# Seven quarter-block products in place of four block products, for two units of a feed-forward layer at a time

## The chip, the cores and the metric

The kernel runs on one core of a Trainium2 chip. The metric is the device time of one execution in microseconds (us), lower is better. The engines are TensorE (PE; its weight loads are shown apart as PEld), VectorE (DVE), ScalarE (ACT), GpSimd (POOL) and SyncE (SP, which here only issues DMAs). Each engine runs its own instructions in order, and waits on semaphores for the others. Matmul results lie in PSUM, in eight banks of 128 partitions x 512 f32; everything else lies in SBUF.

## The reference

`x` is 1,024 tokens of 512 channels. Two layers are added to it, each a conditioner with low-rank adapters followed by a gated feed-forward network:

```
c = down(silu(gate(x)) * up(x))        # conditioner 0: width 1,376, each of its 3 weights plus an adapter per batch
x = x + down(silu(gate(c)) * up(c))    # ffn 0: width 1,792, each weight w * (su @ sv), su and sv of rank 4
l = x @ W.T + b + adapter(x)           # conditioner 1: 512 to 512
x = x + down(silu(gate(l)) * up(l))    # ffn 1: width 1,792, int4 weights with a scale per 128 inputs
```

## The kernel before, in words

Tokens lie on the free axis, in two halves of `TB` = 512; channels lie on the partitions, in four chunks of 128 (`KC`). The hidden width of a layer is cut into *units* of 128: 11 for conditioner 0 (`c`), 14 for ffn 0 (`f`), 14 for ffn 1 (`q`). The program runs through these stages, one after the other: units of `c` (`gate_up` with adapters), `down` of `c` to `h`, units of `f` (`gate_up`), `down` of `f` onto `x`, conditioner 1 (`l_main`, `l_finish`), units of `q`.

**Seven products.** In `c` and `f`, a unit's gate rows and up rows against the two halves of the tokens, and two halves of the input channels, form a 2 x 2 block product, which is done in seven block products in place of eight (in Winograd's arrangement). Product i multiplies a form of the weights, a[i] (128 rows, 256 channels), with a form of the tokens, b[...] (256 channels, 512 tokens). So it is two matmul calls of 128 x 128 weights and 512 columns in f32, and each call leaves two records in the profile. `weight_forms` (L278 to L285) makes s1 = a21 + a22, s2 = s1 - a11, s4 = a12 - s2 and, in the place of a21, s3 = a11 - a21; for `c` from unit 3 on and for `f` it runs on GpSimd (`gate_up_forms`). `token_forms` (L287 to L309) makes T3, T1, T2, T4 on VectorE, once for a layer. `gate_up` (L434 on) does products 1, 6, 7, 5, 3, 2, 4 on TensorE, each into a PSUM bank of its own; ACT copies product 1 (L462), VectorE adds the sums together (L471 to L498), ACT does the SiLU (L495, L499), and GpSimd multiplies gate and up (L497, L502). `down` (L508 on) does the same with pairs of units: its weight forms (`ds`) and token forms (`dt`, L532) are made by VectorE, in the order 1, 2, 3, 7, 5, 6, 4.

**Preparing a unit.** `prepare` loads a unit three ahead (SP's queue) and finishes a unit two ahead. In `f`, `finish_f` (L402 to L420) first makes the scales su @ sv: 12 matmuls (`pw`, 16 rows, 128 columns, f32r, from `scale_parts`, in three banks), which VectorE multiplies into the gate and up weights (L415, twice) and the down weights (L419); then GpSimd makes the forms.

**Conditioner 1** (L852 to L896) is a plain product: four output chunks by two token halves by four input chunks, 32 f32 calls, in PSUM tiles of two banks, plus the low-rank adapter (`low_rank`, `expand`). `l_finish` splits the result into two f32r parts, hi by ACT (L880) and lo by VectorE (L881), which the units of `q` read (L904).

**Order.** A tile is a slot of a pool; a tag with one buffer (`bufs` = 1) is reused only when all readers of its last tile are done. `in_order` pins an instruction behind the one traced before it on its engine; without it the scheduler of the compiler may move an instruction ahead where its operands come early.

Of the kernel before, what the change touches and what calls it, by code (L numbers as in the profile page):

```python
# [7 lines left out]
F32 = mybir.dt.float32  # L8
# [5 lines left out]
P = 128  # L14
# [26 lines left out]
def kernel(  # L41
# [40 lines left out]
    wgu_pool = pool(left0, "wgu", "left", AHEAD + 2)  # L82
# [172 lines left out]
    def expand(banks, b, columns, ts, fresh=(), more=()):  # L255

        for turn in range(len(banks)):
            for tb in range(NTB):  # L260
                i = (turn + tb) % len(banks)
                if banks[i][tb] is None:
                    continue
                rows = bass.ts(tb, P // NTB)
                mm(
                    banks[i][tb], b[rows, columns[i] : columns[i] + P], ts[i][rows, :],
                    start=(i, tb) in fresh, stop=(i, tb) not in more,
                )
# [10 lines left out]
    def weight_forms(engine, a11, a12, a21, a22, s1, s2, s4, pinned=False):  # L279

        in_order(engine.tensor_tensor(s1, a21, a22, ALU.add))
        for to, x1, x2 in ((s2, s1, a11), (s4, a12, s2), (a21, a11, a21)):
            made = engine.tensor_tensor(to, x1, x2, ALU.subtract)
            if pinned:
                in_order(made)  # L285

    def token_forms(pool, name: str, src, pinned: bool, then=None):  # L287
# [9 lines left out]
        for t, x1, x2 in (  # L297
            ("T3", "22", "12"), ("T1", "12", "11"), ("T2", "22", "T1"), ("T4", "21", "T2")
        ):
            b[t] = []  # L300
            for k in range(K2):
                to = pool.tile([P, TB], F32, tag=f"{t}{k}", name=f"{t}_{name}{k}")
# [8 lines left out]
    def product(ps, a, b, start: bool, stop: bool):  # L311
        for n, (w, src) in enumerate(zip(a, b)):
            mm(ps, w, src, start=start and n == 0, stop=stop and n == len(b) - 1)
# [3 lines left out]

    def load_c(f: int, after=None):
        wgu = wgu_pool.tile([P, 2, KC, P], F32, tag="wgu", name=f"wgu_c{f}")
        if after is not None:  # L320
            in_order(nc.vector.tensor_copy(wgu[:, 0, 0, 0:1], after[:, 0:1]))
        if f:
            in_order(nc.sync.dma_start(out=wgu, in_=c_gu[f]))
        wd = wd_pool.tile([P, H], F32, tag="wd", name=f"wd_c{f}")
        ready["c", f] = wgu, wd

    def load_c_down(f: int):
        in_order(nc.sync.dma_start(out=ready["c", f][1], in_=c_down[f]))

    def gate_up_forms(layer: str, f: int, engine):  # L330
        wgu, wd = ready[layer, f][:2]
        s = wgu_pool.tile([P, 3, KC // 2, P], F32, tag="s", name=f"s_{layer}{f}")
        k1, k2 = slice(0, KC // 2), slice(KC // 2, KC)
        g, u = wgu[:, 0], wgu[:, 1]
        weight_forms(engine, g[:, k1], g[:, k2], u[:, k1], u[:, k2], *(s[:, i] for i in range(3)))
        a = {
            1: g[:, k1], 2: g[:, k2], 7: u[:, k1], 4: u[:, k2],
            5: s[:, 0], 6: s[:, 1], 3: s[:, 2],
        }
        ready[layer, f] = {i: [w[:, k] for k in range(KC // 2)] for i, w in a.items()}, wd  # L340

    def finish_c(f: int):
        gate_up_forms("c", f, nc.vector if f < 3 else nc.gpsimd)

# [53 lines left out]
    def load_f(f: int):  # L398
        wgu = wgu_pool.tile([P, 2, KC, P], F32, tag="wgu", name=f"wgu_f{f}")
        in_order(nc.sync.dma_start(out=wgu, in_=f_gu[f]))  # L400
        wd = wd_pool.tile([P, H], F32, tag="wd", name=f"wd_f{f}")
        in_order(nc.sync.dma_start(out=wd, in_=f_down[f]))  # L402
        ready["f", f] = wgu, wd

    def finish_f(f: int):
        wgu, wd = ready["f", f]

        pw = [bank(f"pw_{f}_{s}") for s in range(3)]
        for k in range(KC):
            for s in range(3):  # L410
                rows, ks = slice(s * G, s * G + 4 * RS), bass.ts(k, P)
                sv, su = scale_parts[rows, ks], scale_parts[rows, H + f * P : H + (f + 1) * P]
                mm(pw[s][:, ks], *((su, sv) if s == 2 else (sv, su)), start=True, stop=True)
        for s in range(2):
            nc.vector.tensor_tensor(  # L415
                wgu[:, s].rearrange("p k f -> p (k f)"),
                wgu[:, s].rearrange("p k f -> p (k f)"), pw[s], ALU.mult,
            )
        nc.vector.tensor_tensor(wd, wd, pw[2], ALU.mult)  # L419
        gate_up_forms("f", f, nc.gpsimd)  # L420

    units = [("c", f) for f in range(NF0)] + [("f", f) for f in range(NF)]
    load = {"c": load_c, "f": load_f}
    finish = {"c": finish_c, "f": finish_f}

    def prepare(layer: str, f: int):

        n = units.index((layer, f))
        for ahead, do in ((AHEAD, load), (AHEAD - 1, finish)):
            if n + ahead < len(units):  # L430
                which, at = units[n + ahead]
                do[which](at)
# [4 lines left out]
    def gate_up(  # L437
        act_pool, temps, layer: str, f: int, b, adapters=None, first=False, last=False, between=()
# [3 lines left out]
        a = ready[layer, f][0]  # L442
        mul = (nc.vector if last else nc.gpsimd).tensor_tensor

        def temp(what: str):
            return temps.tile([P, TB], F32, tag=what, name=f"{what}_{layer}{f}", bufs=2)
# [10 lines left out]
        def of(i: int, src: str, stop: bool = True):  # L457
            ps[i] = new(i)
            product(ps[i], a[i], b[src], True, stop)
            return ps[i]  # L460

# [16 lines left out]
        add(u, ps[5], u, ALU.add)  # L478
        for do in between[:1]:
            do()  # L480
        if not first:
            of(3, "22", done)
        for do in between[1:]:
            do()
        if not first:
            of(2, "21", done)
        of(4, "T4", done)
        x2, x3, x4 = ps[2], ps[3], ps[4]

        def finish():  # L490
            if adapters is not None:
                x8 = new(8)
                adapters([[x2, x3], [x4, x8]], {(1, 1)})
            add(p1, x2, p1, ALU.add)
            nc.scalar.activation(p1, p1, AF.Silu)  # L495
# [12 lines left out]
    def down(pool, layer: str, n: int, to, plus: bool, hooks, adapters=None):  # L508
# [11 lines left out]
        for j in range(pairs):  # L520
            wd = [ready[layer, 2 * j + i][1] for i in range(2)]
# [18 lines left out]
        def sums(i: int, m: int, src: str, into=None, start=True, single=None, stop=True):  # L540
# [4 lines left out]
            product(  # L545
                ps, [w[m] for w in a[i]], b[src], start, stop and not alone,
            )
            if alone:
                leftover(ps, m, *single, False, stop)
            return ps  # L550

        def leftover(ps, m: int, row: int, tb: int, start: bool, stop: bool):
            wd = ready[layer, n - 1][1]
            mm(ps, wd[:, bass.ts(m + 2 * row, P)], acts[n - 1, tb], start=start, stop=stop)
# [14 lines left out]
        form("T3", "22", "12", lambda j: pool.tile([P, TB], F32, tag=f"dt{j}", name=f"dt_{layer}{j}"))  # L569
        for m in range(2):  # L570
            nc.scalar.copy(u[m], sums(1, m, "11"))
            if plus:
                nc.gpsimd.tensor_tensor(at(m, 0), at(m, 0), u[m], ALU.add)
        hook(1)
        form("T1", "12", "11", lambda j: b["12"][j])
        for m in range(2):
            ps = sums(2, m, "21", None, True, (0, 0), not more)
            if more:
                extra = bank(f"d8_{layer}{m}")
                leftover(extra, m, 1, 1, True, False)  # L580
                adapters(m, [[ps, None], [None, extra]])
                nc.scalar.copy(at(m + 2, 1), extra)
            nc.vector.tensor_tensor(at(m, 0), ps, at(m, 0) if plus else u[m], ALU.add)
        for m in range(2):
            ps = sums(3, m, "22", None, True, (0, 1), not more)
            if more:
                banks[4, m] = bank(f"d4_{layer}{m}")
                adapters(m, [[None, ps], [banks[4, m], None]], {(1, 0)}, {(1, 0)})
            if plus:
                plus_bank(m, 1, ps)  # L590
            else:
                nc.scalar.copy(at(m, 1), ps)
# [8 lines left out]
        for m in range(2):  # L601
            ps = sums(5, m, "T1")
            plus_bank(m, 1, ps)
            plus_bank(m + 2, 1, ps)
        hook(5)
# [11 lines left out]
    with ExitStack() as c_layer:  # L617
# [7 lines left out]
        w0 = ready["c", 0][0]  # L625

        def load_w0(s: int, ks: slice):
            in_order(nc.sync.dma_start(out=w0[:, s, ks], in_=c_gu[0, :, s, ks]))
# [18 lines left out]
        b_x = token_forms(x_forms, "x", x, True, load_next)  # L647
# [59 lines left out]
        def gate_up_adapters(f: int):  # L707
            def add(banks, fresh):
                for q2 in range(2):
                    for tb in range(NTB):  # L710
                        for s in range(2):
# [4 lines left out]
                                start=(s, tb) in fresh, stop=(s, tb) in fresh or q2 == 1,  # L716
                            )

            return add

# [8 lines left out]
        for f in range(NF0):  # L729
            prepare("c", f)  # L730
# [13 lines left out]
            if f == 8:  # L744
                down_adapters_a.arrange(nc.scalar.copy, slice(0, NB))
            finishing = gate_up(
                act_c, temps, "c", f, b_x, gate_up_adapters(f), f == 0, f == NF0 - 1,
# [21 lines left out]
        def down_adapters(m: int, banks, fresh=(), more=()):  # L769
            expand(banks, b0_down, [m * P, (m + 2) * P], [td[0], td[0]], fresh, more)  # L770
# [7 lines left out]
    with ExitStack() as top:  # L778
        temps = pool(top, "temps_f", "right")
        b_h = token_forms(temps, "h", h, False)  # L780
        for f in range(NF):
            prepare("f", f)
            gate_up(act_f, temps, "f", f, b_h, last=f == NF - 1)()
# [38 lines left out]
    l_adapters.arrange(nc.gpsimd.tensor_copy, slice(0, NB))  # L822
    with ExitStack() as top:
# [20 lines left out]


# [8 lines left out]

    whole, halves = slice(0, T), [bass.ts(tb, TB) for tb in range(NTB)]


    parts = [
# [341 lines left out]
```

## Time and profile before

| | us |
|---|---|
| median of three runs | 705.86 (705.85 to 706.1) |
| the profiled execution | 705.46 |
| its span, first to last instruction | 703.7 |
| units of `c`, from the first product (PE) | 5.1 to 157.3 |
| `down` of `c` | 157.3 to 234.6 |
| units of `f` | 234.6 to 412.2 |
| `down` of `f` | 412.2 to 497.7 |
| conditioner 1 | 497.7 to 532.2 |
| units of `q` and the stores | 532.2 to 703.7 |

Busy in the span: PE 690.1, DVE 394.5, POOL 319.1, ACT 156.3 us. The stages are read from TensorE's timeline, by the tiles that its matmuls write. A line of a timeline gives the start, the duration of the merged records, the engine, the source line, the operation, output and inputs, the shape and how many records were merged; in brackets stands the engine's idle time before it and who ended it. Records of matmuls overlap: a record lasts longer than the distance from one start to the next, so distances of starts are what tells how fast TensorE gets on.

### The profile page before, as it was taken

The numbers are of one execution on the slowest core, as the hardware profiler recorded it, in microseconds if no ns is written. First come the engines' busy times: TensorE is split into PE (matmuls) and PEld (weight loads), VectorE is DVE, ScalarE is ACT, GpSimd is POOL, SyncE is SP. The second block draws the span as 40 slices with busy tenths as digits, with TensorE's granted clock in tenths as the row PEclk, the third lists the DMA queues.
The fourth block names the chain that finished last, engine by engine and source line by source line (L and its number), as shares of the span: only waits on it lengthen the run. The fifth ranks groups of instructions, "written<-read, shape, count | busy, mean of one in ns | idle before, by whom it ended". The sixth has DMA issues, their size and how long they took to land. (4 is left out here: it accounts for less than half of the span.)

```text
span 703.7 us, 6655 instructions
## 1 busy us (share of the span) xinstructions
PE 690.1 (98%) x2362; PEld 359.4 (51%) x2362; DVE 394.5 (56%) x586; ACT 156.3 (22%) x197; POOL 319.1 (45%) x280
## 2 busy tenths in 40 slices
PE   8999999999999999999999999999999999999994
PEld 3444444444344444444444444444446677788872
DVE  6553543449135554555545378513025788999985
ACT  1212112011000011111111110000024555566652
POOL 5357655330010243353443350133202889898885
PEclk9999999999999999999999999999999999999997
DMA  6502152310010021121100020004800120000003
GB/s 229 188 23 89 61 167 81 105 31 1 0 60 1 0 86 49 45 90 45 59 36 0 1 90 1 0 30 135 283 0 31 39 82 16 15 1 0 1 1 119
DMA packets 17180, 40.35 MB, mean 57 GB/s; under 512 B 2990, under 2 KB 4158, under 8 KB 17020
## 3 DMA queue, kind: packets, MB, share of 16 engines
q1 hardware_dynamic: 10476, 23.35, 9.8%
q0 software_dynamic: 5376, 14.49, 6.5%
q10 hardware_dynamic: 1296, 2.10, 0.9%
q8 instruction: 19, 0.31, 0.2%
q14 instruction: 13, 0.11, 0.1%
HBM read 37.83 MB, written 2.10 MB: 57 GB/s over the span
## 5 line engine op out<-in xcount | busy, mean ns | idle before, releaser
L913 DVE SCALAR_TENSOR_TENSOR sum<-gu_q,sg,sum 128x1024 f32<-128x1024 f32 (+1 forms) x75 | 90.4, 1210 | 20.0 <-ACT sum L910 16.3
L904 PE MATMUL gu_q<-h_hi,wgu_q 128*128 128x512 f32 x224 | 89.0, 397 | 1.3 <-ACT sum L910 0.9
L904 PE MATMUL gu_q<-h_lo,wgu_q 128*128 128x512 f32 x224 | 87.4, 390 | 0.0
L913 DVE SCALAR_TENSOR_TENSOR x<-d_q,sd,x 128x1024 f32<-128x1024 f32 (+1 forms) x51 | 54.3, 1087 | 4.0 <-POOL x L919 4.0
L73 PE MATMUL p_f<-h,wgu_f 128*128 128x512 f32 x112 | 53.9, 603 | 0.0
L73 PE MATMUL p_f<-T_h,s_f 128*128 128x512 f32 x112 | 52.6, 592 | 0.0
L73 PE MATMUL p_f<-T_h,wgu_f 128*128 128x512 f32 x112 | 52.6, 592 | 0.0
L910 ACT ACTIVATE sum<-gu_q,sg 128x1024 f32<-128x1024 f32 (+1 forms) x45 | 47.3, 1056 | 22.0 <-PE gu_q L904 21.9
L502 POOL TENSOR_TENSOR act_f<-act_f,u_f 128x512 f32<-128x512 f32 x13 | 16.5, 1269 | 77.5 <-ACT u_f L499 77.5
L919 POOL TENSOR_TENSOR sum<-sum,sum 128x1024 f32<-128x1024 f32 (+1 forms) x15 | 33.9, 2258 | 38.9 <-DVE sum L913 38.2
L904 PEld LDWEIGHTS gu_q<-h_hi,wgu_q 128*128 128x128 f32 x224 | 42.0, 188 | 16.4 <-DVE x L913 3.0
L904 PE MATMUL d_q<-act_hi,wd_q 128*128 128x512 f32 x112 | 45.1, 403 | 3.8 <-ACT y L910 3.3
L904 PEld LDWEIGHTS gu_q<-h_lo,wgu_q 128*128 128x128 f32 x224 | 42.1, 188 | 8.3
L904 PE MATMUL d_q<-act_lo,wd_q 128*128 128x512 f32 x112 | 44.2, 394 | 0.3 <-POOL act_lo L919 0.3
L73 PE MATMUL p_c<-x,wgu_c 128*128 128x512 f32 x88 | 43.0, 613 | 0.0
L919 POOL TENSOR_TENSOR act_lo<-sum,act_hi 128x1024 fp32r<-128x1024 f32 (+1 forms) x15 | 33.8, 2254 | 17.6 <-ACT act_hi L980 16.3
L73 PE MATMUL p_c<-T_x,wgu_c 128*128 128x512 f32 x88 | 41.5, 593 | 0.3 <-DVE T_x L303 0.3
L73 PE MATMUL p_c<-T_x,s_c 128*128 128x512 f32 x88 | 41.2, 592 | 0.0
L73 PE MATMUL d_f<-act_f,ds_f 128*128 128x512 f32 x84 | 36.6, 593 | 0.0
L73 PE MATMUL d_f<-act_f,wd_f 128*128 128x512 f32 x84 | 36.4, 592 | 0.0
L919 POOL TENSOR_TENSOR sum<-sum,sil_q 128x1024 f32<-128x1024 f32 (+1 forms) x15 | 34.0, 2264 | 3.0 <-ACT sil_q L971 2.9
L73 PEld LDWEIGHTS p_f<-T_h,s_f 128*128 128x128 f32 x112 | 21.3, 190 | 26.8 <-issue 26.5
(192 smaller groups left out, 1049.8 us busy)
## 6 DMA issues: line engine op xcount, KB each, us to landing
wgu_f<-in_f_gu_dram SPq DMA_DIRECT2D x14, 512.0 KB
wgu_q<-in_q_gu_dram POOLq DMA_DIRECT2D x14, 512.0 KB, 6.1
wgu_c<-in_c_gu_dram SPq DMA_DIRECT2D x10, 512.0 KB
wd_f<-in_f_down_dram SPq DMA_DIRECT2D x14, 256.0 KB
wd_q<-in_q_down_dram POOLq DMA_DIRECT2D x14, 256.0 KB, 6.3
wd_c<-in_c_down_dram SPq DMA_DIRECT2D x11, 256.0 KB
x<-in_xT_dram ACTq DMA_DIRECT2D x5, 256.0 KB
out_dram<-x SPq DMA_DIRECT2D x5, 256.0 KB
```

Of the source, the lines that this page charges most:

```text
L73: in_order(nc_mm(*args, **kwargs))
L502: mul(act[1], act[1], u, ALU.mult)
L904: nc.tensor.matmul(ps, w, part[:, at], start=(n == 0), stop=(n == len(src) - 1))
L910: in_order(nc.scalar.activation(to, ps, AF.Identity, scale=scale))
L913: nc.vector.scalar_tensor_tensor(to, ps, scale, plus, op0=ALU.mult, op1=ALU.add)
L919: in_order(nc.gpsimd.tensor_tensor(to, a, b, op))
```

## The change

**Two units at a time in `f`.** Units 0 and 1 still run one by one. Units 2 to 13 run as six pairs (`two_units`). Products 1, 6 and 5 stay as they were, for each unit. Products 2, 7, 4 and 3 of both units together are a 2 x 2 block product again (two units by two halves of the channels, two halves of the 512 tokens), and are done in seven products of 128 x 128 weights and 256 columns each (`small`). Their second token forms (`second_tokens`) lie in the place of `x`, which is loaded again afterwards; their second weight forms (`second_forms`) are made by GpSimd for each pair, amid and after the first forms, which are made for two units at once. The quarter results are put together in `r27` and `r43` by ACT copies, in place of some by VectorE, and by accumulation in PSUM banks that already hold another product (`skip_group_check`). The end of a pair (`finish`: last sums, SiLU, multiplies on GpSimd) is issued in the next pair, after its product 1.

**Scales for two units** (`scale_f`): four matmuls of 256 columns and one of 512 for half of the inputs of two units, plus the down weights of one unit, with the same three multiplies on VectorE, which are now 512 elements of two units each.

**Conditioner 1 in seven products**, of two chunks of outputs and 512 columns: 28 f32 calls. Its forms are made by GpSimd during `down` of `f` and its token forms by VectorE, pinned.

**Also**: in `gate_up` products 2 and 3 accumulate onto the banks of products 1 and 5, in the order 1, 6, 7, 5, 4, 2, 3; `down` does so too, in the order 1, 2, 5, 3, 7, 6, 4; the token forms of `h` are pinned, in the order T1, T3, T2, T4, with T3 in the place of the second half of `h`; the first unit of `q` takes its chunks in the order 0, 2, 1, 3; weights lie in tiles of two units.

```diff
-    def weight_forms(engine, a11, a12, a21, a22, s1, s2, s4, pinned=False):
+    def weight_forms(
+        engine, a11, a12, a21, a22, s1, s2, s4, pinned=False, between=None, s3_to=None
+    ):
 
         in_order(engine.tensor_tensor(s1, a21, a22, ALU.add))
-        for to, x1, x2 in ((s2, s1, a11), (s4, a12, s2), (a21, a11, a21)):
+        s3 = (a21 if s3_to is None else s3_to, a11, a21)
+        forms = [(s2, s1, a11), (s4, a12, s2)]
+        forms.insert(0 if between else 2, s3)
+        for n, (to, x1, x2) in enumerate(forms):
             made = engine.tensor_tensor(to, x1, x2, ALU.subtract)
             if pinned:
                 in_order(made)
+            if between and n == 0:
+                between()
...
+    def scale_f(n: int, half: int):
+
+
+        raw, wd = ready["f", "raw", n], ready["f", "down", 2 * n + half]
+        pw = [bank(f"pw_{n}_{half}_{s}") for s in range(3)]
+        rows = [slice(s * G, s * G + 4 * RS) for s in range(3)]
+        of_units = [H + f * P for f in (2 * n, 2 * n + half, 2 * n + 2)]
+        for k in range(2):
+            for s in range(2):
+                mm(
+                    pw[s][:, bass.ts(k, 2 * P)], scale_parts[rows[s], bass.ts(2 * half + k, P)],
+                    scale_parts[rows[s], of_units[0] : of_units[2]], start=True, stop=True,
+                )
+            if k == 0:
+                mm(
+                    pw[2], scale_parts[rows[2], of_units[1] : of_units[1] + P],
+                    scale_parts[rows[2], :H], start=True, stop=True,
+                )
...
         for m in range(2):
-            ps = sums(2, m, "21", None, True, (0, 0), not more)
+            ps = sums(2, m, "21", banks[1, m], False, (0, 0), not more, True)
...
+        for m in range(2):
+            plus_bank(m + 2, 1, sums(5, m, "T1"))
+        hook(5)
         for m in range(2):
-            ps = sums(3, m, "22", None, True, (0, 1), not more)
+            ps = sums(3, m, "22", banks[5, m], False, (0, 1), not more, True)
...
-        b_h = token_forms(temps, "h", h, False)
-        for f in range(NF):
-            prepare("f", f)
-            gate_up(act_f, temps, "f", f, b_h, last=f == NF - 1)()
+        own = own_tiles(temps, "h")
+        b_h = token_forms(
+            lambda t, k: h[k][:, bass.ts(1, TB)] if t == "T3" else own(t, k), h, True,
+            order=("T1", "T3", "T2", "T4"),
+        )
...
+            gate_up_forms(
+                "f", (2 * n, 2 * n + 1), nc.gpsimd, True, lambda: second_forms((2, 7), raw[:, :, 2:6])
+            )
+            second_forms((4,), raw[:, :, 6:8])
+            second_forms((3,), ready["f", "s", n][:, :, 4:6])
+
+        def two_units(n: int, tail):
...
+            def pair(z: str, r, order, between, at):
...
+                both(z1, 1, True)
+                copied(slice(0, 1))
+                both(z5, 5, True)
+                at(0)
+                both(z1, 6, False)
+                copied(slice(1, 2))
+                at(1)
+                both(z1, 7, False)
+                copied(slice(2, 4))
+                at(2)
...
+            def r_tile(what: str, bufs: int = 1):
+                return temps.tile([P, 2, 4, TB // 2], F32, tag=what, name=f"{what}_f{n}", bufs=bufs)
...
+            for u in two:
+                full(b1[u], u, 1, "11")
+                in_order(nc.scalar.copy(p1[:, u], b1[u]))
+            tail()
+            first()
+
+
+            r27 = r_tile("r27")
...
+            def sixth(u: int):
+                b6.append(bank(f"p6_f{n}_{u}"))
+                full(b6[u], u, 6, "T2")
+                add(u_[:, u], b6[u], p1[:, u])
+
+            def amid27(k: int):
+                if k == 0:
+                    small(b1[0], 0, 2, 2, False)
+                else:
+                    sixth(k - 1)
+
+            fifth27 = pair("a", r27, (2, 7), None, amid27)
+            small(b1[0], 1, 2, 3, False)
+            small(b1[1], 0, 2, 4, False)
+            small(b6[0], 0, 7, 2, False)
+            small(b6[0], 1, 7, 3, False)
+            small(b6[1], 0, 7, 4, False)
+            fifth27()
+            c11 = [of_product(r27, 0)[:, bass.ts(u, TB)] for u in two]
+            for u in two:
+                add(c11[u], b1[u], c11[u])
+                in_order(nc.scalar.activation(c11[u], c11[u], AF.Silu))
+            v = [of_product(r27, 1)[:, bass.ts(u, TB)] for u in two]
+            for u in two:
+                add(v[u], b6[u], v[u])
+            add(of_product(r27, 1), of_product(r27, 1), p1.rearrange("p u t -> p (u t)"))
+            then()
+
+            b5 = banks(5)
+            for u in two:
+                full(b5[u], u, 5, "T1")
+                add(act[u][1], b5[u], v[u])
+            last()
...
+            def finish(mul):
+                fifth43()
+                r4, r3 = (of_product(r43, m) for m in two)
+                add(act[0][0], act[0][0], r4[:, :TB])
+                add(act[1][0][:, half], act[1][0][:, half], r4[:, bass.ds(TB, TB // 2)])
+                add(act[1][0][:, other], v[1][:, other], r4[:, bass.ds(TB + TB // 2, TB // 2)])
+                for u in two:
+                    in_order(mul(act[u][0], act[u][0], c11[u], ALU.mult))
+                add(r3, r3, u_.rearrange("p u t -> p (u t)"))
+                for u in two:
+                    c12 = r3[:, bass.ts(u, TB)]
+                    in_order(nc.scalar.activation(c12, c12, AF.Silu))
+                    in_order(mul(act[u][1], act[u][1], c12, ALU.mult))
...
+        for n in range(1, NF // 2):
+            if n + 2 < NF // 2:
+                load_f(n + 2)
+                load_f_down(n + 2)
+            tail = (lambda r: lambda: r(nc.gpsimd.tensor_tensor))(rest_of) if rest_of else nothing
+            rest_of = two_units(n, tail)
+        rest_of(nc.vector.tensor_tensor)
+        for k in range(KC):
+            for tb in range(NTB):
+                load_x(nc.sync, k, tb)
...
+    weight_forms(nc.gpsimd, l11, l12, l21, l22, *(l_forms[:, i] for i in range(3)), True)
...
+    for m in two:
+        in_order(nc.scalar.copy(p1[m], l_sum(1, m, "11")))
+    for m in two:
+        l_sum(7, m, "T3")
```

In `two_units`, `first`, `then` and `last` are the next pair's scales for the first half of the channels, for the second half, and its forms; `add` is a pinned add on VectorE, `full` a product of two 512-column calls.

## The prediction

> **What bounds the kernel now.** I read the page first, then TensorE's timeline through the second feed-forward stage, then the same stretch of GpSimd and VectorE, and last the two seams of that stage. On the page:
>
> ```profile
> PE 690.1 (98%) x2362; PEld 359.4 (51%) x2362; DVE 394.5 (56%) x586; ACT 156.3 (22%) x197; POOL 319.1 (45%) x280
> PEclk9999999999999999999999999999999999999997
> ```
>
> TensorE (PE) works 690.1 of 703.7 us, so a matmul taken away is worth its time, as long as the instructions around it keep up. The timeline of one unit:
>
> ```profile
> 362.65 0.66 PE L73 MATMUL pw<-scale_parts 16*128 16x128 f32 x12
> 363.24 1.98 PE L73 MATMUL p_f<-h,wgu_f 128*128 128x512 f32 x4
> 365.06 1.88 PE L73 MATMUL p_f<-T_h,s_f 128*128 128x512 f32 x4
> 366.78 1.88 PE L73 MATMUL p_f<-T_h,wgu_f 128*128 128x512 f32 x4
> ```
>
> A product is two calls, a call leaves two records, and products start 1.72 us apart (365.06 to 366.78): 0.429 us a record, 0.858 a call, no gaps. Units with scales start 12.80 us apart (235.18, 247.98), the last two without scales 12.12 (376.05, 388.17), so the 12 scale matmuls cost 0.68.
>
> **Fewer matmuls.** In six pairs of units four products (16 calls of 512 columns, 13.73 us) become 28 calls of 256. No row has a 128x128 f32 record of 256 columns. Half of 0.429 is 0.215. The nearest row is the last stage, where one weight load goes with one short record: its records start 0.2265 apart (560.15, 560.37, 560.60). An unhidden pipeline, 0.380 as the 256-column record of pt_d lasts, is the far end. I take 0.2265, 0.453 a call, 12.68 for 28: a pair saves 1.05. Five scale matmuls a half pair instead of twelve a unit: 5/12 of 0.68 by count is 0.28, by columns (1,536 in both) 0.68; I take 0.40 (-0.28 in each of 14). The last conditioner has 28 calls for 32: -3.43. A pair of units alone on TensorE is then 12 x 0.858 + 12.68 + 0.80 = 23.8 us against 25.6. If that were all, the sum would be -14.8 us (four scaled halves in the first conditioner and the first pair -1.12, five pairs -1.8, the last pair, without scales, 23.0 for 24.24, l -3.43).
>
> **What the pair must wait for.** GpSimd (POOL) gets far more to do, in a fixed order:
>
> ```profile
> 248.33 1.27 POOL L497 TENSOR_TENSOR act_f<-act_f,p_f 128x512 f32<-128x512 f32 x1 [1.51 <-DVE act_f L496]
> 249.56 0.72 POOL L281 TENSOR_TENSOR s_f<-wgu_f 128x256 f32<-128x256 f32 x1
> 250.36 0.72 POOL L283 TENSOR_TENSOR s_f<-s_f,wgu_f 128x256 f32<-128x256 f32 x1
> 251.05 0.72 POOL L283 TENSOR_TENSOR wgu_f<-wgu_f 128x256 f32<-128x256 f32 x1
> ```
>
> By starts, 512 elements take 1.23 (248.33 to 249.56), 256 take 0.69, or 0.80 when the operand is the result just before; the line through both gives 0.41 for 128 (estimate), 0.53 when dependent. Forms of the next pair: four of 512 (5.1), four of 256 (3.1), eight of 128 (3.7): 11.9 us against 2 x 2.9 before. They start when the second half of the scales has been applied, and the multiplies of the pair before (four of 512) are queued behind them. But these multiplies read c11, which lies in r27, a tile with one buffer. The next pair's first copy into r27 (ScalarE, ACT) waits for the first two of them, and TensorE's third group (z1, index 6) waits for that copy. The circle per pair, by rows:
>
> - forms on POOL, 11.9;
> - meanwhile VectorE (DVE) adds SBUF to SBUF for the tail: 512, 256, 256, 1024 elements at 0.60, 0.34, 0.34, 1.12 (the rates of ds_f and dt_f below; 1024 by the line through them): 2.4, which don't run beside a POOL add, see next view;
> - two multiplies, 2.5;
> - copy of 512 elements 0.59, and 0.3 for three hand-overs (0.05 to 0.1 each in the rows);
> - PE: two groups (0.91 each) and product 6 of both units (1.72 each), 5.25;
> - DVE: 0.27 to start, the sixth's add 0.60, the fifth's 1.12, four adds 2.4, the long v add 1.12, two scale multiplies 1.2, 0.1 to POOL: 6.8.
>
> Sum 29.7 us a pair; TensorE's own 23.8 lies beside it with 5.9 idle in one piece. That is 4.1 more than 25.6, although no engine is full (PE 23.8, DVE about 19, POOL 16.9). Price of the small calls hardly matters here: only four lie in the circle.
>
> On the 2.4: with POOL and DVE both on SBUF operands the trace has
>
> ```profile
> 419.08 1.50 POOL L573 TENSOR_TENSOR x<-x,du_f 128x512 f32<-128x512 f32 x1 [4.37 <-ACT du_f L571]
> 420.53 0.80 POOL L227 COPY ga<-ga 128x512 f32<-128x512 f32 x1
> ```
>
> ```profile
> 419.49 1.37 DVE L283 TENSOR_TENSOR ds_f<-wd_f,ds_f 128x256 f32<-128x256 f32 x1
> 420.79 0.82 DVE L283 TENSOR_TENSOR wd_f<-wd_f 128x256 f32<-128x256 f32 x1
> 421.54 0.41 DVE L281 TENSOR_TENSOR ds_f<-wd_f,wd_f 128x256 f32<-128x256 f32 x1
> 427.34 4.30 DVE L532 TENSOR_TENSOR dt_f<-act_f,act_f 128x512 f32<-128x512 f32 x7
> 431.56 4.30 DVE L532 TENSOR_TENSOR act_f<-act_f,act_f 128x512 f32<-128x512 f32 x7
> ```
>
> A DVE add of 0.42 takes 1.37, ending just after the POOL instruction: they take turns. Adds with a PSUM operand stay at 0.69 beside POOL. So bounds for the 2.4 are 0 and 2.4; I take 2.4, as the rows show turns.
>
> A stall of 5.9 us may also cost clock. The first four matmuls of the trace (warm) last 1101 ns each for 592, 3.78 us in place of 1.88; no row has an idle stretch of several us later. So 0 to 1.9 a stall; I take 0, because the page's clock row is 9 in every slice but the last. [...]
>
> **The seams.** *Into the stage.* The token forms are now pinned behind the instruction traced before them, the last add of the first down projection, which ends with PE:
>
> ```profile
> 226.93 1.28 DVE L303 TENSOR_TENSOR T_h<-h,h 128x512 f32<-128x512 f32 x2
> ...
> 234.69 0.69 DVE L561 TENSOR_TENSOR h<-d_c,h 128x512 f32<-128x512 f32 x1 [2.87 <-PE d_c L73]
> 235.42 0.69 DVE L303 TENSOR_TENSOR T_h<-h,T_h 128x512 f32<-128x512 f32 x1
> ```
>
> Before, seven of the eight forms ran from 226.93 on, ahead of it. Now five forms of 0.60 (T1, T3, first T2) follow it: ready 3.8 us after the seam, wanted at 1.72: +2.1. *First pair of units, f 0 and 1*: gains only scales. *Pair 1*: its p1 waits for f 1's multiply behind 11.9 us of forms, about +1.2 (0 to 3), so -0.6 net. *Out of it.* Before, VectorE's weight forms began 1.6 us after the last unit and T1's first tile was ready at 432.2, 20.0 after TensorE passed to the down projection at 412.20; nobody needed it early. Now product 5 comes third, at 4 x 6.0 = 24.0, and the last pair's tail (two adds from PSUM, the fifth's, three adds, two multiplies, the long add, and two multiplies that wait for SiLU) ends 7.7 after the last matmul, 6.1 later than 1.6: 26.1. Two POOL adds fall away (about 1.0 each of waiting) and four of the l forms take their place with 1.0 each if they fall here: stall 0 to 4.2, I take 3.5. The reloading of x (eight DMAs on SP) has 18 us until its first reader; hidden. *Last conditioner into the last stage.* The per-block chains (add 0.60, ACT 0.69, DVE 0.75) end some 5 us after the last matmul, 3.1 before: +2.4 (0 to 4), net -1.0. Products 2 and 3 accumulating in the banks of 1 and 5 save DVE adds in the first conditioner and both down projections, none on TensorE's path: 0.
>
> **Sum** against the profiled execution (705.46, its span 703.7): first conditioner's scales -0.6, seam +2.1, f 0 and 1 -0.6, pair 1 -0.6, pairs 2 to 5 4 x 4.1 = +16.4, the last pair 28.9 for 24.24 = +4.7, down projection +3.5, l -1.0: +23.9, 729.4. The median shown, 705.86, lies 0.4 above the profiled one, so 729.8.
>
> **Rivals.**
> 1. *Engines don't block each other*: the circle is 27.3, 12 us less: 717.8. For it: the POOL add beside DVE grew by only 0.24 (1.50 for 1.26).
> 2. *The clock falls in the stalls*: 5 x 1.9 more: 739.3.
> 3. *Faster: the matmuls saved are saved.* Place: first copy into r27. From the second half's scales to the third group there are 11.7 us of other work on TensorE (5.5 to the pair's end, 6.2 after it); if POOL's and ACT's share there, 15.3 here, were below 11.7, nothing waits. Then the pairs give -8.4, and with my seams the sum is -5.6: 700.3 against the median; with all seams hidden too, -14.8: 691.1. For it: TensorE is the only full engine. Against it: POOL's rates scatter by 1%, and the forms alone take 11.9.
> 4. *It doesn't do what it says* (256-column records near 0.38): a pair is 32.4 on TensorE, over 740 with the seams, but then stalls vanish.
>
> **Chances.** Forecast (722 to 736) 0.46; the first rival (709 to 722) 0.17; clock or dear records (736 up) 0.13; faster 0.19; within 0.2%, about what a measurement here can tell from no change, 0.05. Slower 0.76, same 0.05, faster 0.19. The forecast's own range is 722 to 736; to hold 8 in 10 it must reach into both other sides: 697 to 741.
>
> **What would show it.** Right: TensorE idle once a pair before z1, 4 to 6 us, ended by ACT's copy into r27, which waited for POOL's multiply; pairs 29 to 30 us apart; a wait of 2 us on T_h; one on T1 in the second down projection. Wrong: pairs 24 us apart (the third), idle of 3.5 (the first), records of 0.43 us spacing after a stall (the second), 256-column records far from 0.2265.

## The result, and the profile after

The changed kernel takes 742.56 us (median; 740.99 to 742.79), the kernel before 705.89: slower by the ratio 1.0512, 95% interval 1.0499 to 1.0525. The forecast was 729.8 (722 to 736, and 697 to 741 to hold 8 in 10): the direction and the circle were right, two terms put at 0 were not, and the median lies 1.6 us beyond the wide range, while one of the four executions, 740.99, lies at its edge. The profiled execution took 742.53, its span is 740.8.

From the page of the kernel after, TensorE's busy time, its clock by slices, and the group with the longest idle time before it (the idle time follows the second bar, with its releaser and that releaser's part):

```profile
PE 689.1 (93%) x2400; PEld 386.8 (52%) x2400; DVE 439.3 (59%) x624; ACT 183.2 (25%) x237; POOL 361.8 (49%) x324
...
PEclk9999999999999999899999989999999999999998
...
L73 PE MATMUL za_f<-x,s 128*128 128x256 f32 x72 | 23.7, 461 | 27.6 <-ACT r_f L955 27.6
```

TensorE is busy for 689.1 us as before (690.1), although it has fewer columns to work through: where the clock fell the records were longer (2.08 us for 1.10, below), so busy time hides it. The mean granted clock is 0.974, before the change 0.995. TensorE's busy share fell to 93%. The view of the waits of TensorE names the four that the experiments go after (total us, times, longest):

```profile
PE za_f L73 <- ACT r_f L955: 27.6, 6, 6.0
PE d_f L73 <- DVE act_f L595: 4.2, 1, 4.2
...
PE p_f L73 <- DVE T_h L312: 2.2, 1, 2.2
...
PE p_c L73 <- DVE act_c L536: 1.6, 4, 0.7
```

No experiment goes after two other new waits of the last stage: 1.0 us in all on `h_hi` and `h_lo` where it begins, and one of 1.6 us near its end (`gu_q` on `x`, L1282).

The timeline of the kernel after, one pair of units, all engines (PE's weight loads and most lines left out):

```profile
286.12 1.28 POOL L285 TENSOR_TENSOR s_f<-raw_f 128x512 f32<-128x512 f32 x1 [12.78 <-DVE raw_f L470]
...
293.24 2.34 DVE L935 TENSOR_TENSOR act_f<-act_f,r_f 128x512 f32<-128x512 f32 x2
294.39 0.90 POOL L285 TENSOR_TENSOR s<-raw_f 128x128 f32<-128x128 f32 x1
...
296.09 1.47 DVE L935 TENSOR_TENSOR r_f<-r_f,u_f 128x1024 f32<-128x1024 f32 x1
...
296.45 1.43 POOL L290 TENSOR_TENSOR s<-raw_f 128x128 f32<-128x128 f32 x1
...
299.73 2.48 POOL L1060 TENSOR_TENSOR act_f<-act_f,r_f 128x512 f32<-128x512 f32 x2
...
302.24 0.59 ACT L955 COPY r_f<-za_f 128x512 f32<-128x512 f32 x1 [3.43 <-POOL act_f L1060]
302.88 2.08 PE L73 MATMUL za_f<-x,s 128*128 128x256 f32 x4 [5.33 <-ACT r_f L955]
304.75 2.94 PE L73 MATMUL p_f<-T_h,s_f 128*128 128x512 f32 x4
...
308.39 1.88 PE L73 MATMUL p_f<-T_h,s_f 128*128 128x512 f32 x4
...
317.32 1.27 POOL L285 TENSOR_TENSOR s_f<-raw_f 128x512 f32<-128x512 f32 x1 [12.67 <-DVE raw_f L470]
```

The circle of the prediction stands there link by link: forms on GpSimd from 286.12 on, the multiplies by c11 behind them (299.73), which free `r27` for ACT's copy (302.24), which frees the bank for TensorE (302.88, idle for 5.33). Its length is 317.32 - 286.12 = 31.20. What the prediction put at nothing is the clock: after the stall the same four records of `za` take 2.08 for 1.10 in the first pair, and those of product 6 2.94 for 1.88, and the granted clock is 0.50 from 300.04, before the stall's end, to 306.87.

### The profile page after: what moved, and what is told of

It reads as the page before. It is cut to its first block, busy times and chain, and to the rows that moved or that the text cites. A ratio compares the mean times of both kernels' runs of the same rounds, so it can differ in the third digit from the quotient of the medians.

```text
span 740.8 us, 6798 instructions
## 1 busy us (share of the span) xinstructions
PE 689.1 (93%) x2400; PEld 386.8 (52%) x2400; DVE 439.3 (59%) x624; ACT 183.2 (25%) x237; POOL 361.8 (49%) x324
## 5 line engine op out<-in xcount | busy, mean ns | idle before, releaser
L1282 DVE SCALAR_TENSOR_TENSOR sum<-gu_q,sg,sum 128x1024 f32<-128x1024 f32 (+1 forms) x75 | 90.4, 1211 | 20.0 <-ACT sum L1279 15.5
L73 PE MATMUL p_f<-T_h,s_f 128*128 128x512 f32 x112 | 56.9, 642 | 2.2 <-DVE T_h L312 2.2
L1282 DVE SCALAR_TENSOR_TENSOR x<-d_q,sd,x 128x1024 f32<-128x1024 f32 (+1 forms) x51 | 54.3, 1087 | 4.0 <-POOL x L1288 4.0
L73 PE MATMUL za_f<-x,s 128*128 128x256 f32 x72 | 23.7, 461 | 27.6 <-ACT r_f L955 27.6
L73 PE MATMUL p_c<-x,raw_c 128*128 128x512 f32 x88 | 43.1, 614 | 0.0
L73 PE MATMUL d_f<-act_f,ds_f 128*128 128x512 f32 x84 | 38.4, 617 | 4.2 <-DVE act_f L595 4.2
L73 PE MATMUL p_c<-T_x,raw_c 128*128 128x512 f32 x88 | 41.6, 594 | 0.2 <-DVE T_x L312 0.2
L73 PE MATMUL p_f<-h,raw_f 128*128 128x512 f32 (+1 forms) x96 | 41.1, 552 | 0.3 <-ACT p_f L987 0.3
L935 DVE TENSOR_TENSOR u_f<-p_f,p_f 128x512 f32<-128x512 f32 x12 | 8.3, 692 | 55.0 <-issue 32.7
L285 POOL TENSOR_TENSOR s_f<-raw_f 128x512 f32<-128x512 f32 x7 | 9.1, 1299 | 62.4 <-DVE raw_f L470 62.4
L560 POOL TENSOR_TENSOR act_c<-act_c,p_c 128x512 f32<-128x512 f32 x10 | 12.8, 1277 | 52.6 <-DVE act_c L559 44.5
```

Source lines behind the costliest of these rows:

```text
L73: in_order(nc_mm(*args, **kwargs))
L560: mul(act[0], act[0], p1, ALU.mult)
L935: in_order(nc.vector.tensor_tensor(to, x1, x2, ALU.add))
L1282: nc.vector.scalar_tensor_tensor(to, ps, scale, plus, op0=ALU.mult, op1=ALU.add)
```

## The experiments

Each is the changed kernel with the edit shown. Where a kernel has a single time, the trace is the evidence and the time only supports it, since the kernel after itself scatters by 1.8 us.

**Undo the circle: keep c11 elsewhere** (timed in several runs).

```diff
-            c11 = [of_product(r27, 0)[:, bass.ts(u, TB)] for u in two]
+            quarters = [of_product(r27, 0)[:, bass.ts(u, TB)] for u in two]
+            c11 = [both[0] for both in pair_acts(n + 1)] if n + 1 < NF // 2 else quarters
             for u in two:
-                add(c11[u], b1[u], c11[u])
+                add(c11[u], b1[u], quarters[u])
```

`pair_acts(n + 1)` are the next pair's result tiles, allocated one pair early.

> The changed kernel, with the gate sums c11 of a pair kept in the activation tiles of the next pair in place of r27, so that r27 is free once VectorE and ScalarE are done with it; nothing else moves. My theory (the circle through r27 and GpSimd's queue): the wait of 5.3 us before the third group of z1 goes in all five pairs and the slowed records after it too; pairs start 23.5 us apart (23.2 to 24.2) in place of 30.8 to 31.2; total 742.6 - 5 x 7.4 = 705.5 (702 to 710). Rival (the forms themselves come too late, r27 only hides it): TensorE waits at the next reader of GpSimd's results, s of products 2 and 7 or product 6; pairs 26 to 29, total 715 to 732.

Measured: 716.6 us, ratio to before 1.0154 (1.0137 to 1.0171), pairs 25.75 apart. So 26 us go with one link of the circle, but the time lies above the 702 to 710 expected: another wait, of 1.87 in pairs 2 to 5 and 2.49 in the last, came in its place. The timeline of this kernel around it:

```profile
294.57 1.47 DVE L942 TENSOR_TENSOR r_f<-r_f,u_f 128x1024 f32<-128x1024 f32 x1
...
296.14 1.15 ACT L1072 ACTIVATE r_f<-r_f 128x512 f32<-128x512 f32 x2 [2.27 <-DVE r_f L942]
...
297.19 0.57 ACT L962 COPY r_f<-za_f 128x512 f32<-128x512 f32 x1
...
297.39 0.46 POOL L290 TENSOR_TENSOR s<-s_f,s 128x128 f32<-128x128 f32 x1
297.80 0.45 POOL L290 TENSOR_TENSOR s<-s_f 128x128 f32<-128x128 f32 x1
...
297.90 1.10 PE L73 MATMUL za_f<-x,s 128*128 128x256 f32 x4 [1.87 <-POOL s L290]
```

The releaser listed is GpSimd, but these two GpSimd results (made from `s_f`, for product 3) aren't what the four matmuls read, and the second ends after they start. The bank `za` they write is freed by the copy of 297.19. That copy could have run from 294.8 on, when the first `za` group (293.61, 1.13 long) had ended, but stood in ACT's queue behind two SiLUs of the pair before, which waited for VectorE. A new theory, tested below.

**Fill the stall with matmuls** (one run): six calls into a bank that nobody reads, in pairs 2 to 6.

```diff
                     small(b1[0], 0, 2, 2, False)
+                    if n > 1:
+                        filler = bank(f"filler_f{n}")
+                        for _ in range(6):
+                            mm(filler, a[0][1][0], b_h["11"][0], start=True, stop=True)
```

> The changed kernel, with six extra calls of 128x512 into a bank that nobody reads, put on TensorE where it waits in pairs 2 to 6 (5.1 us a pair, less than the wait). Theory (idle TensorE loses clock): the stretch from the third group of z1 to the end of product 6 takes 5.2 us again in place of 6.8 to 7.2, pairs are 1.6 to 2.0 shorter, 29.1 apart, total 733 to 735. Rival (these records are slow because their operands come late, not for the clock): same pairs, total 741 to 743.

Measured: 733.03 us, pairs 29.25 apart; more work on TensorE, and 9.5 us less (8.3 in the pairs and 1.7 behind the T_h wait, see the last section, less 0.5 behind `down` of `f`). TensorE's timeline in this kernel:

```profile
295.64 5.31 PE L73 MATMUL filler_f<-h,raw_f 128*128 128x512 f32 x12
301.13 1.13 PE L73 MATMUL za_f<-x,s 128*128 128x256 f32 x4 [0.18 <-ACT r_f L955]
302.10 1.88 PE L73 MATMUL p_f<-T_h,s_f 128*128 128x512 f32 x4
```

With TensorE kept at work the records behind have their old lengths, 1.13 and 1.88 (2.08 and 2.94 in the kernel after), and the mean granted clock of the run is 0.993 (0.974). The clock loss is caused by the idle stretch and lies in the circle itself, since VectorE's adds wait for these matmuls.

**Banks of their own for products 2 and 3 in conditioner 0** (one run), as before the change.

```diff
         if first:
             x2, x3 = ps[2], ps[3]
+        elif layer == "c":
+            x2, x3 = of(2, "21", done), of(3, "22", done)
         else:
             onto(2, "21", 1)
```

The sums, SiLU and adapters that follow from it go back to their old form with it.

> The changed kernel, with products 2 and 3 of the first conditioner's units in banks of their own again and VectorE's two adds back, in the new order of products. Theory (product 3 on the bank of product 5 waits for VectorE's add, which waits behind the split of the scales): the four waits of 0.7 us on act_c in units 2 to 6 go, the down projection starts 2.2 to 2.7 us earlier, at 157.3; total 740. Rival (later loads at the start): it starts at 159.5 to 160 as before.

Measured: 740.37 us. The waits on `act_c` are gone (one of 0.7 and three of 0.3, not four of 0.7), and `down` of `c` starts at 158.03 instead of 159.80 (157.33 before the change): 1.8 us, less than the theory's 2.2 to 2.7, but more than the rival allows.

**h not pinned** (one run): the argument `pinned` of `token_forms` for `h` is False, as before the change.

```diff
-            lambda t, k: h[k][:, bass.ts(1, TB)] if t == "T3" else own(t, k), h, True,
+            lambda t, k: h[k][:, bass.ts(1, TB)] if t == "T3" else own(t, k), h, False,
```

> The changed kernel, with the token forms of h not pinned; the compiler then puts six of the eight ahead of the last two adds of the down projection. Theory (pin, then clock): the wait of 2.2 us on T_h goes, and the 1.8 us that the next records took longer go with it; unit 0 takes 13.3 in place of 17.4; total 738.5. Rival (a wait of 2 us costs only itself): unit 0 takes 15.2, total 740.4.

Measured: 737.75 us; the wait on `T_h` is gone, and unit 0 of `f` takes 13.28 us in place of 17.38. That is 4.1 less for a wait of 2.17; the difference is clock again: in the kernel after the granted clock behind this wait was 0.50 and the two groups of four records there took 2.77 and 2.81 us (last section), here each takes 1.88.

**l's weight forms issued later** (one run): the same four GpSimd instructions written into the hook behind product 5.

```diff
-    weight_forms(nc.gpsimd, l11, l12, l21, l22, *(l_forms[:, i] for i in range(3)), True)
+
+    def l_weight_forms():
+        weight_forms(nc.gpsimd, l11, l12, l21, l22, *(l_forms[:, i] for i in range(3)), True)
+
+    def after_fifth():
+        turn_scales()
+        l_weight_forms()
+
     with ExitStack() as top:
-        down(pool(top, "down_f", "right"), "f", NF, x, True, {5: turn_scales})
+        down(pool(top, "down_f", "right"), "f", NF, x, True, {5: after_fifth})
```

> The changed kernel, with the subtractions on GpSimd that make the last conditioner's weight forms issued after the fifth product of the feed-forward's down projection instead of ahead of the projection. Theory: VectorE's weight forms of the down projection take 0.83 to 1.49 us instead of 0.42 because they take turns with those of GpSimd, and this makes act_f late; then the wait of 4.24 us inside the down projection falls below 0.5 us, the clock cost behind it (1.7 us) goes too, and the time is about 736.7 us. Rival: VectorE's tail of the last pair makes act_f late; then the wait falls by less than 1 us and the time stays above 741 us.

Measured: 739.77 us, the wait unchanged. The experiment failed for a plain reason, seen in the timeline of this kernel:

```profile
454.74 0.66 POOL L227 COPY ga<-ga 128x512 f32<-128x512 f32 x1 [1.72 <-issue]
455.37 1.42 POOL L285 TENSOR_TENSOR l_forms<-lw 128x512 f32<-128x512 f32 x1
...
470.71 4.51 PE L73 MATMUL d_f<-act_f,ds_f 128*128 128x512 f32 x6 [4.25 <-DVE act_f L595]
```

The forms still run right behind the copy of `ga`, as in the kernel after. GpSimd had nothing else to do there, so the later place in the program delayed nothing. So this run decides nothing about the wait, and its 2.8 us below the kernel after are clock for the most part: 1.7 behind the T_h wait (last section) and 0.9 in the pairs.

**All four edits so far** (one run).

> Four edits of the changed kernel at once: c11 in the next pair's tiles, banks of their own for the conditioner c's second and third product, h not pinned, l's weight forms late. If their stalls are separate, the gains add: 716.6 from the first alone, less 2.2, 4.8 and 5.9, is about 704 us, with pairs still 25.7 us apart. Rival: the stalls hide one another, and the sum falls short by over 3 us (over 707 us).

Measured: 710.56 us. By the number the rival; but the 5.9 us counted for l's forms were never saved (the wait of 4.1 is still there), and without them the sum was 716.6 - 2.2 - 4.8 = 709.6. Within 1 us the stalls add up, but not row by row: of the 4.8 counted for T_h, 1.8 is clock that the profiled execution with c11 moved had not lost there; it had lost 1.7 behind the stall of its last pair instead (26.80 us for that pair, here 25.12).

**The previous pair's SiLUs behind the copies** (several runs), on top of c11 moved.

```diff
-            tail()
+            gated = tail()
             first()
...
                 else:
                     sixth(k - 1)
+                if k == 2 and gated:
+                    gated()
```

`gated` holds the two SiLUs and the two multiplies behind them, that ended `finish`; now they come after the three copies of `z1`.

> The kernel with c11 in the next pair's tiles, and the previous pair's two last SiLUs and the multiplications behind them issued after the copies of z1 on ScalarE's queue, not ahead of them. Theory: the wait of 1.87 us a pair that was left is the copy of z1 standing in ScalarE's queue behind two SiLUs that wait for VectorE; then the wait goes, pairs stand about 23.9 us apart, and the time is 716.6 - 10 = about 706.5 us. Rival: GpSimd's weight forms, which the trace lists as the releaser, are late themselves; then the wait of 1.8 us stays and the time is 715 to 717 us. Third case: the next wait on VectorE or GpSimd takes its place within the pair, 24.5 to 25.5 us a pair and 709 to 714 us.

Measured: 705.74 us (703.84 to 707.75; the profiled execution is the slowest, with a clock loss behind T_h, where eight records take 5.58 us for 3.76), ratio to before 0.9998 (0.9988 to 1.0007), pairs 23.65 apart, no wait within the pairs 2 to 6. The timeline of this kernel:

```profile
296.94 0.58 ACT L962 COPY r_f<-za_f 128x512 f32<-128x512 f32 x1 [0.95 <-PE za_f L73]
...
298.00 1.03 PE L73 MATMUL za_f<-x,s 128*128 128x256 f32 x4
...
299.50 0.46 POOL L290 TENSOR_TENSOR s<-s_f,s 128x128 f32<-128x128 f32 x1
...
302.55 1.15 ACT L1076 ACTIVATE r_f<-r_f 128x512 f32<-128x512 f32 x2
```

GpSimd begins the first of the two forms named above 1.5 us after TensorE's group has started: they were not its releaser, ACT's queue was.

**All five edits** (several runs).

> All five edits at once: c11 in the next pair's tiles, the SiLUs behind the copies, banks of their own in the conditioner c, h not pinned, l's weight forms late. If the gains add, about 706.5 - 2.2 - 4.8 - 5.9 = 693.5 us, 1.7% below the kernel before the change. Rival: the products were saved against stalls that only move; then no version comes below the 705.9 us of before.

Measured: 699.93 us, ratio 0.9919 (0.9903 to 0.9936). Again the 5.9 of l's forms are missing; without them the sum was 699.4.

**l's weight forms on VectorE, all else as in the last kernel** (several runs).

```diff
-        weight_forms(nc.gpsimd, l11, l12, l21, l22, *(l_forms[:, i] for i in range(3)), True)
+        weight_forms(nc.vector, l11, l12, l21, l22, *(l_forms[:, i] for i in range(3)), True)
```

> The kernel with all five edits, but the last conditioner's weight forms made by VectorE after the down projection's fifth product, where it had over 5 us of nothing to do, and not by GpSimd. Now GpSimd makes none while VectorE makes the projection's. Theory: taking turns cost VectorE 4 to 5 us there; then its five instructions of 0.71 to 1.49 us take 0.42 again, the wait of 4.11 us for act_f is gone, and the time is 694 to 696 us. Rival one: VectorE's late tail makes act_f late; then the wait stays over 3 us and the time is 699 to 701. Rival two: VectorE's four instructions more make the T2 form of the sixth product late by up to 3 us; 697 to 699.

Measured: 693.87 us, ratio 0.9832 (0.9815 to 0.9848): the fastest version, 11.8 us below the kernel before (705.66 in the same comparison). The timelines of the kernel after and of this one, around the wait for act_f:

```profile
458.18 1.42 POOL L285 TENSOR_TENSOR l_forms<-lw 128x512 f32<-128x512 f32 x1
458.51 1.37 DVE L290 TENSOR_TENSOR ds_f<-ds_f,wd_f 128x256 f32<-128x256 f32 x1
459.68 1.33 POOL L290 TENSOR_TENSOR l_forms<-l_forms,lw 128x512 f32<-128x512 f32 x1
459.92 1.37 DVE L290 TENSOR_TENSOR ds_f<-wd_f,ds_f 128x256 f32<-128x256 f32 x1
...
473.51 4.94 PE L73 MATMUL d_f<-act_f,ds_f 128*128 128x512 f32 x7 [4.24 <-DVE act_f L595]
```

```profile
416.45 0.41 DVE L285 TENSOR_TENSOR ds_f<-wd_f,wd_f 128x256 f32<-128x256 f32 x1
416.90 0.43 DVE L290 TENSOR_TENSOR ds_f<-ds_f,wd_f 128x256 f32<-128x256 f32 x1
...
425.43 4.30 DVE L597 TENSOR_TENSOR act_f<-act_f,act_f 128x512 f32<-128x512 f32 x7
426.26 12.25 PE L73 MATMUL d_f<-act_f,ds_f 128*128 128x512 f32 x28
```

Starts tell it: in the first fence VectorE and GpSimd begin by turns, each 1.4 to 1.5 us after its last; in the second VectorE's adds take 0.41 to 0.43 and TensorE doesn't wait (its 28 calls before end as the first form is there, so the cover is used up).

**The same edit alone** (one run).

> The changed kernel with this one edit alone: l's weight forms on VectorE after the fifth product. Theory of turns: wait for act_f gone (4.24 before), with the slower clock behind it, 742.5 - 5.9 is about 736.6 us, give or take the 1.5 us by which the clock behind the stalls varies. Rival, the late tail: the wait stays over 3 us and the time is 740 us or more.

Measured: 736.23 us, the wait 0.20 instead of 4.24, with VectorE's tail as long as before: the turns made act_f late, the tail alone did not.

## Why the prediction came out as it did

By its own terms, predicted and measured, in us of the profiled executions (differences of starts on TensorE's timeline; before the change a unit is counted from its scale matmuls):

| term | predicted | measured |
|---|---|---|
| conditioner 0 (`c`), units | -0.6 | +2.5 |
| seam into `f`, with f 0 and 1 | +1.5 | +3.7 |
| pair 1 | -0.6 | -0.8 |
| pairs 2 to 5 | +16.4 | +21.4 |
| last pair | +4.7 | +6.1 |
| `down` of `f` | +3.5 | +6.2 |
| conditioner 1 and last stage | -1.0 | -1.9 |
| sum | +23.9 | +37.1 (the spans; the rows give 37.1) |

- **The circle** has every link where the prediction put it. Predicted 29.7, measured 31.20 in the pair shown: forms with turn-taking 13.61 (14.3 predicted: turns cost 1.7, not 2.4, if the forms alone take the 11.9 estimated), multiplies to the copy 2.51 (2.5), copy and hand-over 0.64 (0.89), TensorE 7.23 (5.25), VectorE 7.21 (6.8). So the link that was mis-sized is TensorE's, and its 1.98 are clock.
- **"I take 0, because the page's clock row is 9 in every slice but the last"** is the step that failed. The row was read from a kernel without such stalls, so it couldn't tell the cost of one; the upper bound of 1.9 stood beside it and was the better choice. Group 6 and product 6 of both units take 5.23 us without a stall ahead (273.67 to 278.90, pair 1) and 7.23, 6.95, 6.86, 6.81, 6.78 behind the five stalls: 8.5 us. With 1.8 behind the wait for T_h and 1.7 behind that for act_f the clock cost 12.0 us. The sum fell short by 13.2: the clock's 12.0 and 3.1 in `c`, less 1.9 by which the other terms came out cheaper. Filling the stall showed the cause. The second rival, 739.3, had this term (9.5), but no other.
- **"None on TensorE's path: 0"**, for products 2 and 3 accumulating onto the banks of 1 and 5, failed too: product 3 now waits until VectorE has read product 5's bank (`act_c`, L536), in four units of `c`, behind VectorE's other work. Of the 3.1 us by which this stage missed, own banks gave 1.8 back; the cause of the rest is open.
- **The seam T_h**: 2.17 for 2.1 predicted; of the remaining 2.1 by which that row was missed, 1.8 are clock.
- **`down` of `f`**: the wait was 4.24, the upper bound (4.2), where I took 3.5: the GpSimd forms of l did fall there, four of them, and five VectorE adds took turns with them. 1.7 more is clock.
- **Price of the small calls**: 0.431 us a call (records 0.2155 apart), not 0.453. As the prediction said it mattered little while the circle ruled. Without the circle it does: with the SiLUs moved, pairs are 23.65 apart for 23.8 computed and 25.6 before.
- **The scales** were priced too low: the unit that starts at 376.05 has its scale matmuls just ahead of it, at 375.46. The two units without any start at 388.17 and 400.19, 12.02 apart, so twelve scale matmuls cost 0.79, not 0.68, and the last pair took 24.03 before the change, not 24.24. This matters little.
- **The third rival**, matmuls saved are saved, named the place correctly, the first copy into r27. Its condition, shorter shares of GpSimd and ACT, was not met in the kernel after; the later kernels take GpSimd's multiplies out of the circle and put ACT's queue in another order instead. With the waits at the seams gone as well the kernel runs in 693.87 us, where "all seams hidden too" said 691.1. The matmuls were worth their time all along: TensorE is busy for 674.9 us in that kernel, 15.2 less than before the change at the same mean granted clock (0.995), where the prediction counted 14.8. By that count the kernel after paid some 14.8 + 37.1 = 51.9 in waits and slow clock, an estimate.

The granted clock fell to 0.50 at all five stalls of 5.3 to 6.0 us (from 300.04, 334.18, 364.90, 395.62 and 422.92 on), and behind the wait of 2.17 (from 242.02 on); not every run lost time behind that wait (last section).

Where VectorE and GpSimd worked on SBUF operands at the same time, both took longer: in the kernel after 1.37 us for 0.42 for an add of 128x256 on VectorE (458.51 and 459.92; 456.97), and 1.43 for 0.45 for one of 128x128 on GpSimd (296.45; 299.32).

## What to carry to other kernels

Before saving matmuls on a full TensorE, follow each reused tile and bank once around (who must have read it, and what stands ahead of that reader in its queue): an engine that is idle 40% of the time can still set the period, as GpSimd with 18.6 us of work (13.6 and twice 2.5) in a pair of 31 did here. Price a stall on TensorE of several us at its length plus the slow matmuls behind it (1.6 to 2.0 us each for the five here), and do so even if the profile at hand shows no slow clock, since it shows no stall either. When a stall has gone, look at the next one in the same place by the readiness of every operand and bank, not by the releaser's name alone.

## What the runs showed of the hardware that was not expected

The same wait of 2.17 us at the same place costs clock in some executions and none in others. The matmuls behind it, in the kernel after and in the one with c11 moved:

```profile
241.01 2.77 PE L73 MATMUL p_f<-T_h,s_f 128*128 128x512 f32 x4 [2.17 <-DVE T_h L312]
243.57 2.81 PE L73 MATMUL p_f<-h,raw_f 128*128 128x512 f32 x4
```

```profile
241.21 1.96 PE L73 MATMUL p_f<-T_h,s_f 128*128 128x512 f32 x4 [2.17 <-DVE T_h L312]
243.00 1.88 PE L73 MATMUL p_f<-h,raw_f 128*128 128x512 f32 x4
```

Eight matmul records take 5.58 us in the first and 3.84 in the second, 1.8 and 0.1 more than the 3.76 of the kernel with h not pinned, which has no wait there. Of the seven profiled kernels that keep this wait, these two among them, four had a loss of 1.8 and three one of 0.1: the length of an idle stretch alone doesn't decide it, so a single run can be off by that much, and the profiled executions with c11 moved and with the filled stall each have 1.7 us of their gain from it.

In the kernel after the granted clock reads 0.50 behind this wait, from 242.02 to 245.43, and ahead of the last stage from 300.04, 334.18, 364.90, 395.62 and 422.92 (the five stalls) and 474.12 (the wait for act_f) besides, for 3.41 us each time but twice that from 300.04 and from 422.92. Around the wait for T_h it reads as follows (stretch, its length, TensorE's busy time and instructions, granted clock; then DMA):

```profile
core 0: us, PE busy (x), PEclk, DMA share, GB/s
238.60:242.02 3.42, 1.25 (x4) 1.00 0.00 0
242.02:245.43 3.41, 3.41 (x6) 0.50 0.02 5
```

So the clock fell 1.01 us after TensorE had started again (241.01), with the records already running. What decides between a loss of 1.8 and one of 0.1 behind the same wait is not shown by these runs.
